# Layer 0 of a four-layer graph network on one core: the first chunk's norm taken in two pairs of tiles

## The chip, the cores and the metric

One Trainium2 chip, one of its cores. The metric is the device time of one execution of the whole kernel in microseconds (us); several executions are summed up by their median.

## The reference, cut to what matters

The kernel runs four layers over `x` (128 sequences of 64 nodes with 256 features, fp32). Each layer is `x = x + layer(relu(layernorm(x)))`. The change lies in the first stage of layer 0 alone:

```python
h = jnp.maximum(_layernorm(x, axis=-1), 0.0)
# layer 0
h = jax.nn.relu(jnp.einsum('ts,bsh->bth', adj, h @ Wg0 + bg0))
h = jax.nn.relu(jnp.einsum('ts,bsh->bth', adj, h @ Wg1 + bg1))
# then four LSTMs over windows of 1, 2, 3 and 4 nodes of h, and the residual
```

Layers 1 to 3 (attention over edges, a graph convolution with batch norm, attention over all nodes) are not touched.

## The kernel before, in words

The 8192 tokens are cut into 16 chunks of 512, each held as a tile `xin` of 128 partitions x 4 tiles x 256 features. `graph_convolutions(n)` is a generator that takes chunk n through layer 0's two graph convolutions in five stages, with a `yield` after each; the loop behind it advances several chunks by one stage per turn, so that their stages interleave. The stages of a chunk:

1. The norm. On VectorE (DVE) `bn_stats` and `bn_aggr` for each of the four tiles (L96, L97); on ScalarE (ACT) one square root over the four variances (L104); on DVE a reciprocal (L105) and one `scalar_tensor_tensor` that makes the bias (L106); on ACT four `Relu` activations with scale and bias (L120, `scaled`). The result is `h`.
2. `aggregate`: 8 matmuls of `h` with the block matrix `bdA` (two copies of the transposed adjacency) on TensorE (PE, L51), and two DVE copies of 128x512 out of PSUM into `aggT` (L171).
3. Four matmuls with `Wg0` (L51, `bank<-aggT,wg`); for each half a DVE operation (L624) that adds `rsum` times `bg0` and a `Relu` on ACT (L632), giving `h1T`.
4. Eight matmuls with `Wg1` and two DVE additions of `bg1` (L647).
5. Eight matmuls with `bdA`, two `Relu` on ACT (L663) into the tile that the LSTMs read.

An fp32 matmul of the program shows as two MATMUL records in the profile.

Ahead of chunk 0 PE runs products of a tile of ones with itself (`turn_over`, L57: 4 matmuls, then the row sums of the adjacency into a PSUM bank at L600, then 8 more); DVE copies the row sums out into `rsum` (L602).

The loads. SyncE's queue (SP) issues, in order: the four tiles of chunk 0 (L576), chunk 1 (L569), `Wg0` (L582), `Wg1` (L586), chunks 2 and 3 (L569), two LSTM biases (L591, L592), chunk 4, and then what the tables of layer 1 need: first `acol` (L308, 1 KB), then eight small pieces `ahalf` (L313), the edge lists, further chunks. ACT's queue issues the adjacency, transposed (`adjT`, two halves) and plain (`adj`, two halves, L579), `bg0` (L584, 1 KB) and `bg1` (L588, one row of 1 KB read for each of the 128 partitions). Chunk 4 goes into the buffer of chunk 0, so its load is issued when the last of chunk 0's four activations at L120 has read it. The loads of SP and ACT take eight semaphores in turn, and a load waits until the eighth load before it has landed.

The tables of layer 1 (`edge_tables`) are built by DVE operations that are strewn between those of the graph convolutions. Among them is `diag_a` at L346, two operations that multiply the identity by a column of `acol`.

Order on an engine: the framework's scheduler places instructions; those given to `late` (`keep_in_program_order`) keep their order among themselves. Each engine runs its own list strictly in order and waits at an instruction until its semaphores are there. The statistics (`stats`) and the activations (`scaled`) of the norms are kept in program order; the roots (L104 to L106), the copies L171 and the table operations are placed by the scheduler.

Of the kernel before, what the change touches and what calls it, by code (L numbers as in the profile page):

```python
# [9 lines left out]
F32 = mybir.dt.float32  # L10
# [3 lines left out]
AF = mybir.ActivationFunctionType  # L14
ALU = mybir.AluOpType
AX = mybir.AxisListType

P = 128
T = 64
# [12 lines left out]
def gnn_stack_kernel(ctx: ExitStack, tc: tile.TileContext, a: dict, out: bass.AP):  # L32
    nc = tc.nc
# [6 lines left out]
    stat = ctx.enter_context(tc.tile_pool(name="stat", bufs=4))  # L40
# [3 lines left out]
    def bank():  # L44
        return psums["now"].tile([P, 512], F32, tag="bank", name="bank", bufs=psums["banks"])
# [4 lines left out]
    def mm(o, lhsT, rhs, start=True, stop=True):  # L50
        nc.tensor.matmul(o, lhsT, rhs, start=start, stop=stop)  # L51

    def turn_over(lhsT, rhs, times):

        p = bank()
        for _ in range(times):
            late(nc.tensor.matmul(p[:, : rhs.shape[-1]], lhsT, rhs, start=True, stop=True))  # L57
# [17 lines left out]
    eps = const.tile([P, 1], F32, tag="eps", name="eps")  # L75
    nc.vector.memset(eps, 1e-5)

    def late(ins):

        tc.keep_in_program_order(ins)  # L80
# [4 lines left out]
    class Norm:  # L85
# [13 lines left out]
        def roots(self):  # L99
            mv = self.mv  # L100
            rs = self.rs = stat.tile([P, 4], F32, tag="ln_rs", name="ln_rs")
            nm = self.nm = stat.tile([P, 4], F32, tag="ln_nm", name="ln_nm")
            if self.root_on_scalar:
                nc.scalar.activation(rs, mv[:, :, 1], AF.Sqrt, bias=eps)  # L104
                nc.vector.reciprocal(rs, rs)  # L105
                nc.vector.scalar_tensor_tensor(nm, mv[:, :, 0], -1.0, rs, ALU.mult, ALU.mult)  # L106
            else:
                first = nc.gpsimd.tensor_scalar(rs, mv[:, :, 1], 1e-5, None, ALU.add)
                if self.known:
                    self.keep(first)  # L110
                nc.gpsimd.tensor_tensor(rs, rs, half_power, ALU.pow)
                nc.gpsimd.tensor_tensor(nm, mv[:, :, 0], rs, ALU.mult)
                nc.gpsimd.tensor_scalar(nm, nm, -1.0, None, ALU.mult)

        def scaled(self, i):

            if self.h is None:
                self.h = hpool.tile([P, 4, D], F32, tag="h", name="h")
            self.keep(
                nc.scalar.activation(  # L120
                    self.h[:, i, :],
                    self.xt[:, i, :],
                    AF.Relu,
                    bias=self.nm[:, i : i + 1],
                    scale=self.rs[:, i : i + 1],
                )
            )
# [37 lines left out]
    def aggregate(h, bd, dst):  # L165

        for c in range(2):
            p = bank()
            for i in range(4):
                mm(p[:, i * P : (i + 1) * P], h[:, i, c * P : (c + 1) * P], bd)  # L170
            nc.vector.tensor_copy(dst[:, c, :], p)  # L171
# [314 lines left out]
    with ExitStack() as l0:  # L486
# [60 lines left out]
        bias = w0.tile([P, MAX_SKIP, 8], F32, tag="bias", name="bias")  # L547
        bias2 = w0.tile([P, MAX_SKIP, 8], F32, tag="bias2", name="bias2")
        ones = w0.tile([P, P], F32, tag="ones", name="ones")
# [4 lines left out]
        with ExitStack() as conv:  # L554
# [12 lines left out]
            def load_x(n):  # L567
                xt = xin.tile([P, 4, D], F32, tag="xin", name="xin")
                nc.sync.dma_start(out=xt, in_=token_tiles(a["x"], n))  # L569
                return xt  # L570
# [10 lines left out]
            wg0 = wc.tile([P, 2, D], F32, tag="wg0", name="wg0")  # L581
            nc.sync.dma_start(out=wg0, in_=a["Wg0"])  # L582
            bg0 = wc.tile([P, 2], F32, tag="bg0", name="bg0")
            nc.scalar.dma_start(out=bg0, in_=a["bg0"])  # L584
            wg1 = wc.tile([P, 2, D], F32, tag="wg1", name="wg1")
            nc.sync.dma_start(out=wg1, in_=a["Wg1"])  # L586
            bg1 = wc.tile([P, D], F32, tag="bg1", name="bg1")
            nc.scalar.dma_start(out=bg1, in_=a["bg1"].partition_broadcast(P))  # L588
            for n in (2, 3):
                coming[n] = load_x(n)  # L590
            nc.sync.dma_start(out=bias, in_=a["bih"])  # L591
# [6 lines left out]
            rsum = wc.tile([P, T], F32, tag="rsum", name="rsum")  # L598
            p = bank()
            late(nc.tensor.matmul(p[:, :T], ones[:T, :], adjT2[:T, :], start=True, stop=True))  # L600
            turn_over(ones, ones, 8)
            nc.vector.tensor_copy(rsum, p[:, :T])  # L602
            rsum_b = rsum.unsqueeze(1).to_broadcast([P, 8, T])

            def graph_convolutions(n):

                norm = Norm(coming.pop(n), True)
                for i in range(4):
                    norm.stats(i)
                    if n == 1 and i == 1:  # L610
                        yield
                h = norm.finished()
                if 4 <= n + 3 < NCH:
                    coming[n + 3] = load_x(n + 3)
                yield
                aggT = g0.tile([P, 2, CHUNK], F32, tag="aggT", name="aggT")
                h1T = g0.tile([P, 2, CHUNK], F32, tag="h1T", name="h1T")
                aggregate(h, bdA, aggT)
                yield
                for c in range(2):  # L620
                    p = bank()
                    for k in range(2):
                        mm(p, wg0[:, k, c * P : (c + 1) * P], aggT[:, k, :], k == 0, k == 1)
                    nc.vector.scalar_tensor_tensor(  # L624
                        h1T[:, c, :].rearrange("p (b t) -> p b t", t=T),
                        rsum_b,
                        bg0[:, c : c + 1],
                        p.rearrange("p (b t) -> p b t", t=T),
                        ALU.mult,
                        ALU.add,  # L630
                    )
                    nc.scalar.activation(h1T[:, c, :], h1T[:, c, :], AF.Relu)  # L632
                yield
                z = aggT.rearrange("p c t -> p (c t)").rearrange("p (i d) -> p i d", i=4)
                for ip in range(2):
                    p = bank()
                    for i2 in range(2):
                        i = 2 * ip + i2
                        for k in range(2):
                            mm(  # L640
                                p[:, i2 * D : (i2 + 1) * D],
                                h1T[:, k, i * P : (i + 1) * P],
                                wg1[:, k, :],
                                k == 0,
                                k == 1,
                            )
                    nc.vector.tensor_tensor(  # L647
                        z[:, 2 * ip : 2 * ip + 2, :],
                        p.rearrange("p (i d) -> p i d", i=2),
                        bg1.unsqueeze(1).to_broadcast([P, 2, D]),  # L650
                        ALU.add,
                    )
                yield
                if n < NCH // 2:
                    col = n % 2 * CHUNK
                    dst = hTs0[n // 4][:, n % 4 // 2, :, col : col + CHUNK]
                else:
                    dst = hop.tile([P, 2, CHUNK], F32, tag="hop", name="hop")
                for c in range(2):
                    p = bank()  # L660
                    for i in range(4):
                        mm(p[:, i * P : (i + 1) * P], z[:, i, c * P : (c + 1) * P], bdA)
                    nc.scalar.activation(dst[:, c, :], p, AF.Relu)  # L663
                if n >= NCH // 2:
                    nc.sync.dma_start(out=hmem[n], in_=dst)
# [341 lines left out]
        for slot in range(len(tasks) + 2):  # L1007
# [33 lines left out]
            if new:  # L1041
# [4 lines left out]
                if step.w == MAX_SKIP and step.t == 2 and k < 2 and step.g < NGR - 1:  # L1046
                    for u in range(2):
                        n = 4 * step.g + 2 * u + k
                        later.append((slot, "x", n))
            while later and later[0][0] <= slot:  # L1050
                _, kind, n = later.pop(0)
# [28 lines left out]
    with ExitStack() as l1:  # L1080
# [32 lines left out]
        for g, c, u, ip in last_outs:  # L1113
            if not ip:
                n = 4 * g + 2 * u + c
# [523 lines left out]
    with ExitStack() as l2:  # L1639
# [55 lines left out]
        with ExitStack() as dense2:  # L1695
# [67 lines left out]
            with ExitStack() as first_dense:  # L1763
# [43 lines left out]
                for slot, (pr, m2) in enumerate(tasks):  # L1807
                    n = slot + 3
                    if slot == NCH - 5:
# [3 lines left out]
                            out=early[:, 0, : 2 * P].rearrange("p (q m) -> p q m", q=2),  # L1813
                            in_=a["W2T"].rearrange("p (q k) (j m) -> p k q j m", q=2, j=2)[:, 0, :, 1, :],
# [569 lines left out]
```

## Time and profile before

| what | us |
|---|---|
| three runs | 1938.48, 1938.86, 1939.79 |
| median | 1938.86 |
| the profiled execution's own time | 1934.87 |
| its span, first to last instruction | 1933.1 |
| PE busy in it | 1909.7 (99%) |
| DVE, ACT, GpSimd (POOL) busy | 1320.9, 1166.4, 435.7 |

The profiled execution is 3.99 us below the median of the three runs. Rows of the timeline read: start in us from the span's start, duration in us, engine, source line, operation, output <- inputs, shape, count, and in brackets the engine's idle time before the row and what ended it. An engine with the letter q (SPq, ACTq) is its queue issuing a DMA. PEld is PE's weight load, which overlaps with PE.

### The profile page before, as it was taken

Reading aid. Unit: us, or ns where it says so; the run is one execution under the profiler, and the core shown is the slowest. Engines: PE = TensorE matmul, PEld = TensorE weight load, DVE = VectorE, ACT = ScalarE, POOL = GpSimd, SP = SyncE. Lnnn points to the kernel's source line nnn. Section 1 sums busy time; section 2 is a strip of 40 time slices with the busy share of each in tenths; the row PEclk is TensorE's granted clock in tenths of the full one; section 3 lists DMA queues with packets and bytes.
Section 4 is the critical chain, followed back from the end, with each engine's and each line's share of the span. In section 5 each row is a group of like instructions: output and inputs, shape, how many; then the busy total and the mean of one; then the engine's idle time right before and its main releaser. Section 6 shows DMA issues by size and latency. Waiting matters only on the chain. (4 is left out here: it accounts for less than half of the span.)

```text
span 1933.1 us, 25259 instructions
## 1 busy us (share of the span) xinstructions
PE 1909.7 (99%) x9146; PEld 1395.2 (72%) x9146; DVE 1320.9 (68%) x2531; ACT 1166.4 (60%) x2200; POOL 435.7 (23%) x622
## 2 busy tenths in 40 slices
PE   9999999999999999999999999999999999999998
PEld 7777468876678874688766788876676875444787
DVE  8774675674565557755745655688788877787886
ACT  4353775664565547756645656488886656592654
POOL 0333021110010000211100100066776520000584
PEclk9999999999999999999999999999999999999999
DMA  8846010010010035100100100242323841022112
GB/s 278 297 170 219 0 39 0 1 77 0 1 77 1 1 135 203 39 1 1 77 0 1 61 1 16 96 171 95 136 69 116 326 162 57 1 77 78 43 66 88
DMA packets 67212, 158.25 MB, mean 82 GB/s; under 512 B 6928, under 2 KB 41872, under 8 KB 64784
## 3 DMA queue, kind: packets, MB, share of 16 engines
q1 hardware_dynamic: 60272, 127.87, 18.8%
q0 software_dynamic: 6208, 28.58, 4.0%
q8 instruction: 72, 1.18, 0.2%
q14 instruction: 52, 0.43, 0.1%
q10 hardware_dynamic: 608, 0.20, 0.1%
HBM read 98.95 MB, written 57.68 MB: 81 GB/s over the span
## 5 line engine op out<-in xcount | busy, mean ns | idle before, releaser
L800 PE MATMUL pa<-xop,wih 128*128 128x256 f32 (+2 forms) x1376 | 442.8, 412 | 2.3 <-DVE gate L854 1.9
L828 ACT ACTIVATE gate<-gate,bias 128x256 f32<-128x256 f32 (+2 forms) x368 | 247.8, 678 | 170.6 <-DVE gate L844 86.8
L800 PEld LDWEIGHTS pa<-xop,wih 128*128 128x128 f32 x1376 | 259.2, 190 | 87.7 <-issue 19.8
L800 PE MATMUL pa<-lstm_h,whh 128*128 128x256 f32 (+1 forms) x896 | 283.6, 398 | 0.0
L800 PE MATMUL pc<-xop,wih 128*128 128x256 f32 (+2 forms) x736 | 251.1, 423 | 0.0
L844 DVE TENSOR_TENSOR gate<-pb,gate 128x256 f32<-128x256 f32 (+2 forms) x184 | 87.6, 476 | 228.2 <-PE pb L800 159.5
L800 PEld LDWEIGHTS pa<-lstm_h,whh 128*128 128x128 f32 x896 | 170.2, 190 | 40.2
L772 POOL COPY xop<-hT 128x256 f32<-128x256 f32 (+1 forms) x36 | 30.0, 833 | 655.2 <-DVE gate L851 278.8
L800 PEld LDWEIGHTS pc<-xop,wih 128*128 128x128 f32 x736 | 139.8, 190 | 51.2 <-issue 22.5
L861 DVE TENSOR_TENSOR gate<-pc,gate 128x256 f32<-128x256 f32 (+2 forms) x184 | 87.8, 477 | 117.7 <-PE pc L800 116.8
L1210 ACT ACTIVATE lr<-pair 128x1024 f32<-128x1024 f32 x128 | 124.2, 1023 | 39.9 <-ACT xv L1194 16.8
L800 PE MATMUL pc<-lstm_h,whh 128*128 128x256 f32 (+1 forms) x448 | 141.8, 398 | 0.0
L843 ACT COPY gate<-pa 128x256 f32<-128x256 f32 (+2 forms) x184 | 76.0, 413 | 86.7 <-PE pa L800 86.5
L1175 PE MATMUL bank<-wlv,hT 128*128 128x260 f32 x480 | 115.6, 382 | 1.7 <-DVE xq L1186 1.7
L854 DVE TENSOR_TENSOR gate<-pa,gate 128x256 f32<-128x256 f32 (+2 forms) x184 | 87.7, 476 | 41.2 <-PE pa L800 40.5
L828 ACT ACTIVATE gate<-pa,bias 128x256 f32<-128x256 f32 (+2 forms) x184 | 93.8, 510 | 30.6 <-PE pa L800 28.4
L848 ACT COPY gate<-pa 128x256 f32<-128x256 f32 (+2 forms) x184 | 75.2, 409 | 56.2 <-PE pa L800 55.3
L800 PE MATMUL pb<-xop,wih 128*128 128x256 f32 (+1 forms) x320 | 101.7, 399 | 1.4 <-POOL xop L772 1.2
L1175 PEld LDWEIGHTS bank<-wlv,hT 128*128 128x128 f32 x480 | 88.2, 190 | 16.6 <-DVE xq L1186 3.6
L800 PEld LDWEIGHTS pc<-lstm_h,whh 128*128 128x128 f32 x448 | 85.1, 190 | 20.1
L851 ACT COPY gate<-pc 128x256 f32<-128x256 f32 (+2 forms) x136 | 57.9, 426 | 53.2 <-PE pc L800 53.1
L1216 DVE SCALAR_TENSOR_TENSOR lr<-lr,fold 128x1024 f32<-128x1024 f32 x64 | 82.7, 1293 | 3.7 <-ACT lr L1210 1.7
(391 smaller groups left out, 3706.5 us busy)
## 6 DMA issues: line engine op xcount, KB each, us to landing
wih<-qih SPq DMA_DIRECT2D x6, 1792.0 KB, 10.5
field<-keep SPq DMA_DIRECT2D x4, 2304.0 KB, 11.1
whh<-qhh SPq DMA_DIRECT2D x5, 1792.0 KB, 7.2
xres<-in_x SPq DMA_DIRECT2D x16, 512.0 KB, 4.7
xa<-xres POOLq DMA_DIRECT2D x16, 512.0 KB, 4.0
xin<-xb SPq DMA_DIRECT2D x16, 512.0 KB, 3.3
h<-xb SPq DMA_DIRECT2D x16, 512.0 KB, 3.3
xin<-in_x SPq DMA_DIRECT2D x15, 512.0 KB, 5.8
```

What stands on the lines that cost most here:

```text
L772: copy(self.as_nodes(v[:, to : to + 1]), self.nodes(slice(k, k + 1), t))
L800: ins = nc.tensor.matmul(p[:, : self.N], weights[kind, self.phase](k, q), x[k], start=first_ and kind == "ih", stop=kind == "hh" or not se ...
L828: nc.scalar.activation(out, in_, AF.Tanh if q == 2 else AF.Sigmoid, bias=bias[:, self.w - 1, 2 * q + j : 2 * q + j + 1],)
L843: nc.scalar.copy(blk[0, 0], pa[:, :N])
L844: nc.vector.tensor_tensor(blk[0, 0], pb[:, :N], blk[0, 0], ALU.add)
L848: nc.scalar.copy(blk[1, 0], pa[:, :N])
L851: (nc.vector.tensor_copy if not self.t and self.w > 1 else nc.scalar.copy)(blk[1, 1], pc[:, :N])
L854: nc.vector.tensor_tensor(blk[1, 1], pa[:, :N], blk[1, 1], ALU.add)
L861: nc.vector.tensor_tensor(blk[1, 0], pc[:, :N], blk[1, 0], ALU.add)
L1175: ins = nc.tensor.matmul(o, hTs[n][:, k, i * P : (i + 1) * P], wlv[:, k, cols], start=k == 0, stop=k == 1)
L1210: nc.scalar.activation(lr, p, AF.Relu)
L1216: late(nc.vector.scalar_tensor_tensor(lrs[1], lrs[0], fold, lrs[1], ALU.mult, ALU.add))
```

## The change

For chunk 0 alone the norm is written out: the statistics of tiles 0 and 1, one square root over these two, the statistics of tile 2, reciprocal and bias of the first pair, activation 0, the statistics of tile 3, the square root of the second pair, activation 1, reciprocal and bias of the second pair, activations 2 and 3, all kept in program order. The copy of `rsum` is put behind them and kept in order too. The second `turn_over` has 6 matmuls in place of 8. `bg0` and `bg1` are issued by GpSimd's queue instead of ACT's.

```diff
+        def root_pair(self, ip, part):
+            if ip + part == 0:
+                self.rs = stat.tile([P, 4], F32, tag="ln_rs", name="ln_rs")
+                self.nm = stat.tile([P, 4], F32, tag="ln_nm", name="ln_nm")
+            i2 = slice(2 * ip, 2 * ip + 2)
+            rs, nm, mv = self.rs[:, i2], self.nm[:, i2], self.mv[:, i2]
+            if part == 0:
+                self.keep(nc.scalar.activation(rs, mv[:, :, 1], AF.Sqrt, bias=eps))
+            else:
+                self.keep(nc.vector.reciprocal(rs, rs))
+                self.keep(nc.vector.scalar_tensor_tensor(nm, mv[:, :, 0], -1.0, rs, ALU.mult, ALU.mult))
...
-            nc.scalar.dma_start(out=bg0, in_=a["bg0"])
+            nc.gpsimd.dma_start(out=bg0, in_=a["bg0"])
...
-            nc.scalar.dma_start(out=bg1, in_=a["bg1"].partition_broadcast(P))
+            nc.gpsimd.dma_start(out=bg1, in_=a["bg1"].partition_broadcast(P))
...
-            turn_over(ones, ones, 8)
-            nc.vector.tensor_copy(rsum, p[:, :T])
+            turn_over(ones, ones, 6)
+            rsum_bank = p
...
-                for i in range(4):
-                    norm.stats(i)
-                    if n == 1 and i == 1:
-                        yield
-                h = norm.finished()
+                if n == 0:
+                    norm.stats(0)
+                    norm.stats(1)
+                    norm.root_pair(0, 0)
+                    norm.stats(2)
+                    norm.root_pair(0, 1)
+                    norm.scaled(0)
+                    norm.stats(3)
+                    norm.root_pair(1, 0)
+                    norm.scaled(1)
+                    norm.root_pair(1, 1)
+                    norm.scaled(2)
+                    norm.scaled(3)
+                    h = norm.h
+                    late(nc.vector.tensor_copy(rsum, rsum_bank[:, :T]))
+                else:
+                    for i in range(4):
+                        norm.stats(i)
+                        if n == 1 and i == 1:
+                            yield
+                    h = norm.finished()
```

The built programs differ in order over the first 130 or so of DVE's instructions and nowhere behind them; PE's list differs by the two matmuls left out, and in that chunk 0's eight matmuls of `aggregate` stand half by half instead of tile by tile. On DVE the scheduler now places the first `diag_a` ahead of chunk 1's last `bn_aggr`, and the second between chunk 1's reciprocal and its bias:

```
before: bn_stats, bn_aggr, L624, reciprocal L105, bias L106, bn_stats, diag_a, bn_aggr, bn_stats, L624, bn_aggr, bn_stats, diag_a
after:  bn_stats, diag_a, bn_aggr, L624, reciprocal L105, diag_a, bias L106, bn_stats, bn_aggr, bn_stats, L624, bn_aggr
```

The rows begin with the statistics of chunk 1's last tile. On SP's queue the order of the first 20 loads stays, but two loads fewer take part in the turn of the eight semaphores: chunk 1 now waits for the first half of `adjT` instead of chunk 0's first tile, and `acol` for chunk 1 instead of `bg1`. On GpSimd the two loads stand ahead of the copies that fill `bdA` (L595).

## The prediction

> **What bounds the kernel now.** I read the page first, then PE's waits and timeline over the first 45 us, then the timelines of DVE, ACT and SP there, then the DMA view in stretches.
>
> ```profile
> PE 1909.7 (99%) x9146; PEld 1395.2 (72%) x9146; DVE 1320.9 (68%) x2531; ACT 1166.4 (60%) x2200; POOL 435.7 (23%) x622
> ```
>
> PE is the bound; only its idle time can be won or lost. PE's waits of the first 150 us:
>
> ```profile
> PE bank L57 <- DVE ones L550: 1.2, 1, 1.2
> PE bank L51 <- ACT h L120: 0.8, 2, 0.5
> PE bank L51 <- DVE aggT L171: 0.6, 1, 0.6
> PE bank L424 <- DVE wide L420: 0.2, 1, 0.2
> PE bank L51 <- ACT h1T L632: 0.2, 1, 0.2
> ```
>
> PE's rows place them: all but the 0.2 us at L424 end by 17.25, and from there PE runs without a gap for 70 us.
>
> ```profile
> 3.81 3.65 PE L57 MATMUL bank<-ones 128*128 128x128 f32 x16
> 7.97 2.09 PE L51 MATMUL bank<-bdA,h 128*128 128x128 f32 x16 [0.51 <-ACT h L120]
> 10.63 3.70 PE L51 MATMUL bank<-aggT,wg 128*128 128x512 f32 x8 [0.56 <-DVE aggT L171]
> 14.61 0.71 PE L51 MATMUL bank<-bdA,h 128*128 128x128 f32 x4 [0.28 <-ACT h L120]
> 17.25 3.29 PE L51 MATMUL bank<-wg,h1T 128*128 128x256 f32 x14 [0.16 <-ACT h1T L632]
> ```
>
> So the price of this change is how much later or earlier PE reaches the row at 17.25; all behind it moves along. What feeds these rows on DVE (and, last two rows, ACT):
>
> ```profile
> 7.94 0.43 DVE L96 BATCH_NORM_STATS2 ln_st<-xin 128x6 f32<-128x256 f32 x1 [0.75 <-DMA xin<-in_x]
> 9.88 1.29 DVE L171 COPY aggT<-bank 128x512 f32<-128x512 f32 x2 [0.16 <-PE bank L51]
> 12.65 0.75 DVE L624 SCALAR_TENSOR_TENSOR h1T<-rsum,bg,bank 128x512 f32<-128x512 f32 x1 [0.28 <-PE bank L51]
> 13.31 0.17 DVE L105 RECIPROCAL ln_rs<-ln_rs 128x4 f32<-128x4 f32 x1
> 15.20 0.29 DVE L346 TENSOR_SCALAR diag_a<-ident,acol 128x128 f32<-128x128 f32 x1 [1.18 <-DMA acol<-in_a]
> 15.40 0.18 DVE L97 BATCH_NORM_AGGREGATE ln_mv<-ln_st 128x2 f32<-128x6 f32 x1
> 15.49 0.40 DVE L96 BATCH_NORM_STATS2 ln_st<-xin 128x6 f32<-128x256 f32 x1
> 13.43 0.63 ACT L632 ACTIVATE h1T<-h1T 128x512 f32<-128x512 f32 x1 [0.73 <-DVE h1T L624]
> 13.97 2.06 ACT L120 ACTIVATE h<-xin,ln_nm,ln_rs 128x256 f32<-128x256 f32 x4
> ```
>
> Two waits for loads stand here: chunk 1's data at 7.94 and `acol` at 15.20. The second costs little now, because all that chunk 1's matmuls at 14.61 need is ahead of it. The DMA totals from 7 to 9.5 us with its two queues (q10 is ACT's), then from 9.5 to 14:
>
> ```profile
> DMA packets 454, 0.59 MB, mean 237 GB/s; under 512 B 46, under 2 KB 284, under 8 KB 454
> q1 hardware_dynamic: 307, 0.46, 50.8%
> q10 hardware_dynamic: 147, 0.13, 30.9%
> DMA packets 1875, 1.51 MB, mean 336 GB/s; under 512 B 462, under 2 KB 1844, under 8 KB 1875
> ```
>
> The DMA is a backlog: `acol`, issued at 9.79, lands 5.4 us later, just behind chunk 4 (issued 9.33, 5.7 us).
>
> **Chunk 0's norm.** The two issues of 0.60 and 0.44 us leave ACT's queue, so the table load of 1.28 us starts at 3.25 instead of 4.36 and ends at 4.53. Tile 0 lands at 2.9 (issued at 0.72, 2.2 us), DVE is through its long memsets at 2.82; two tiles of statistics at some 0.6 us each with a memset between (4.06 to 5.22 before) are done at 4.4. Root 4.53 to 4.83; from its end to the first activation it was 0.44 (6.79 to 7.23), plus 0.2 for the third tile's statistics in between: activation 0 at 5.5. Tile 3's statistics end about 6.0; the second root runs behind activation 0 to 6.35, plus 0.44: activation 2 at 6.8, activation 3 from 7.3 to 7.9. It ended at 9.30 before: 1.4 us earlier. The two matmuls left out (4 of 16 records in 3.65 us, 0.9 us) ran in PE's waiting time; PE then starts at 6.5 and has half 0 done by 8.3 instead of 9.8.
>
> **Where that gain goes.** On DVE the `aggT` copies stand behind chunk 1's first statistics, four table operations and the `rsum` copy, and those statistics wait for chunk 1's load. In the rows that is 7.94 to 9.72, with 0.16 us idle before the copies at 9.88. So the copies can come at most 0.16 us earlier however early PE is. Chunk 1's load now waits for the `adjT` half (in at 3.16, where PE's L600 starts at 3.19) and not for tile 0: issued at 3.2 instead of 2.98, it lands near 8.1. Copies at 10.0, `Wg0` matmuls at 10.75 instead of 10.63. The 1.4 us shrink to -0.1 or +0.1. The second, small extra root, reciprocal and bias (0.30, 0.18, 0.16 us) lie in the same cover.
>
> **The wait that moves forward.** After the copies (1.3 us), two rows of statistics: DVE is at the first `diag_a` at about 12.3, and there it now stands ahead of chunk 1's last `bn_aggr`, of L624, reciprocal and bias, which release ACT's root, its `Relu` L632 and chunk 1's activations, which release PE. From `acol`'s landing A: `diag_a` 0.20 to the next row (15.20 to 15.40), `bn_aggr` 0.1: L624 at A+0.3. It ends at A+1.05, L632 starts at A+1.08 (12.65 to 13.43 was 0.78). The bias L106 comes at A+1.24: L105 0.66 after L624 (12.65 to 13.31), then 0.28 for the second `diag_a` between. Activation 0.54 behind L632 (13.43 to 13.97): A+1.62. PE 0.64 behind it (13.97 to 14.61): A+2.26. The 0.16 us at 17.25 are absorbed, as the second L624 is not held again. So PE's shift is A + 2.26 - 0.16 - 14.61 = A - 12.51.
>
> **When `acol` lands.** It is queued behind chunk 4, whose issue comes earlier (activation 3 ends at 7.9, not 9.30), but the backlog sets the end. Upper end: the same bytes over the same engines, A = 15.2, shift +2.7. Lower end: from 5.2 us, 2.65 MB (chunks 1 to 4, `Wg0`, `Wg1`, biases) at the best slice's 385 GB/s take 6.9, and 0.9 us lie between the last data and the landing (14.3 to 15.2): A = 13.0, shift +0.5. In between: with q10 gone from 7 to 9.5, where `bg1` was read, q1 could move 336 GB/s x 2.5 us = 0.84 MB instead of 0.46, worth 1.1 us, less the 0.2 of chunk 1's later issue. A = 14.3, shift **+1.8**. I take that, as it is nearest to rows of this stretch. Behind 17.25 the feeding operations keep their leads over PE (`aggT` ready at 18.98, needed at 20.37; the next activations start at 19.22, needed at 23.81), and DVE is held less long than PE is shifted, so nothing is added.
>
> **GpSimd's queue.** Two issues of 0.53 to 0.80 us (the first three of its kind, at 78.6 us) stand ahead of the `bdA` copies at 3.28 and 3.99, in idle time of 1.46 us, and PE wants `bdA` at 6.5: nothing, until each takes 2 us more. `bg0` is first read by L624 near 14.6, `bg1` by L647 near 21 (19.40 before): ten us of cover.
>
> **The clock.** The 16 dummy records up to 7.46 take 3.65 us, 16 of the same shape at 23.81 take 1.95: PE starts at half rate and is fast by 8 us. The change makes PE idle from 14.3 to 16.6, 2.3 us, where the longest idle time of before is the 1.2 us of the first wait shown; whether the rate falls, no row shows. Bounds: nothing, or as long a slow stretch as at the start, 1.19 to some 7.2, 6 us at half rate, 3.0 us lost. I take nothing, since 2.3 is nearer to the gaps of up to 1.2 behind which rows keep their length.
> The Trainium skill ("TensorE: Matmul & The Clock Gate", section "HAM oscillation") asks for no PE-idle gaps over some 3.4 us; by that rule 2.3 us would cost nothing, and a gap past it would add an estimated 1.7 us (half of one 3.4 us window).
>
> **Sum.** 1934.87 + 1.8 = 1936.7 for the profiled execution; carried to the median of the runs, 3.99 higher: 1938.86 + 1.8 = **1940.7**. That is 0.09%; about 0.2% (3.9 us) is what a measurement of this kernel can tell from no change.
>
> **Rivals.**
> *No hold*: `acol` lands before DVE asks for it (12.3), or chunk 1's load comes before 7.8. Then -0.1 to, at the very most, the 1.4 us by which `h` is early: 1937.5 to 1938.8. For it: q10 leaves q1 alone. Against it: the lower bound of A is 13.0. Chance 0.10.
> *Slow clock*: the forecast's hold, and PE falls to half rate behind it: +1.8 + 3.0 = +4.8, 1943.7. It decides once the slow stretch is over 4.2 us (2.1 us lost). For it: PE's lead-in is shorter by 0.9 us and its idle time twice the longest of before. Chance 0.14.
> *The change doesn't do what it says*: chunk 0's `h` is not early because `bg1` on the DMA engines from 2 to 4 us delays tiles 2 and 3. Up to 1.0 us of delay leaves the forecast as it is, since the copies wait for chunk 1; beyond, `Wg0` and with it nothing before A is late. Price 0.
>
> **How the numbers follow.** Forecast 0.76 (A from 13.0 to 15.2: 1939.4 to 1941.6, and a us on each side, as three runs spread over 1.3). The range of 1938.0 to 1943.7 takes in the slow clock's centre and leaves out most of *no hold*. Faster by over 0.2%: 0.03. Slower: 0.17, the slow clock and a part for what the rows don't show. Same: 0.80.
>
> **What would show it.** `h` done near 7.9 and the `aggT` copies still near 10; DVE idle some 2 us before `diag_a`, ended by `acol` near 14.3; PE idle over 2 us before chunk 1's matmuls near 16.6; no new gap behind. Wrong if DVE isn't held there, if PE's 128x512 records behind the hold are over 0.6 us apart, or if the shift at 45 us differs from that at the end.

## The result and the profile after

| what | before | after |
|---|---|---|
| median of the runs on one chip | 1939.05 (22 runs) | 1941.92 (22 runs) |
| lowest and highest | 1938.48, 1942.29 | 1940.63, 1945.63 |
| the profiled execution's own time | 1934.87 | 1941.91 |
| its span | 1933.1 | 1940.1 |

The ratio of the times is 1.0014, with an interval of 1.0008 to 1.002: the change costs 1.6 to 3.9 us, 2.9 by the medians. That is below the 0.2% that the prediction took for what a measurement can tell, but the whole interval is on the slow side. The profile shows where it is lost. Line numbers are higher now: by 13 for the loads, the copies (L184), `diag_a` (L359) and the activations that make `h` (L133), by 29 for L653 (L624 before).

PE's two waits that grew, in its waits from 0 to 150 us (us in total, times, longest):

```profile
PE bank L51 <- ACT h L133: 2.7, 2, 1.8
PE bank L51 <- DVE aggT L184: 1.7, 1, 1.7
```

They were 0.8 and 0.6. PE's timeline of the kernel after places them:

```profile
7.93 2.41 PE L51 MATMUL bank<-bdA,h 128*128 128x128 f32 x14 [0.87 <-ACT h L133]
12.08 3.70 PE L51 MATMUL bank<-aggT,wg 128*128 128x512 f32 x8 [1.74 <-DVE aggT L184]
17.60 0.71 PE L51 MATMUL bank<-bdA,h 128*128 128x128 f32 x4 [1.82 <-ACT h L133]
19.92 3.19 PE L51 MATMUL bank<-wg,h1T 128*128 128x256 f32 x14
26.38 1.95 PE L51 MATMUL bank<-bdA,h 128*128 128x128 f32 x16
```

The last of these rows is chunk 2's. Before it was:

```profile
23.81 1.95 PE L51 MATMUL bank<-bdA,h 128*128 128x128 f32 x16
```

`Wg0` starts at 12.08 instead of 10.63, chunk 1's matmuls at 17.60 instead of 14.61. Chunk 2's start at 26.38 instead of 23.81, and that 2.57 us stays the shift of PE's rows for hundreds of us; below I call it the steady shift. It compares one profiled execution with another. What feeds them on DVE, and the last of chunk 0's activations on ACT:

```profile
6.41 0.43 DVE L96 BATCH_NORM_STATS2 ln_st<-xin 128x6 f32<-128x256 f32 x1 [0.83 <-DMA xin<-in_x]
9.41 0.43 DVE L96 BATCH_NORM_STATS2 ln_st<-xin 128x6 f32<-128x256 f32 x1 [1.49 <-DMA xin<-in_x]
11.34 1.28 DVE L184 COPY aggT<-bank 128x512 f32<-128x512 f32 x2
15.38 0.29 DVE L359 TENSOR_SCALAR diag_a<-ident,acol 128x128 f32<-128x128 f32 x1 [1.90 <-DMA acol<-in_a]
7.29 1.61 ACT L133 ACTIVATE h<-xin,ln_nm,ln_rs 128x256 f32<-128x256 f32 x3
```

Three loads are late here. Tile 3 of chunk 0 comes at 6.41, so `h` is done at 8.90: 0.4 us earlier than before, not 1.4. Chunk 1 comes at 9.41 (7.94 before). And DVE stands at `diag_a` for 1.90 us until `acol` lands. The DMA view from 4 to 6.5 us shows what competes with the first two (queue: packets, MB, share of the 16 engines). Before, then after, where q0 is GpSimd's queue:

```profile
q1 hardware_dynamic: 493, 0.49, 75.4%
q10 hardware_dynamic: 126, 0.02, 4.2%
```

```profile
q0 software_dynamic: 45, 0.13, 46.2%
q1 hardware_dynamic: 320, 0.31, 40.6%
```

`bg1` is read in this stretch now, and SP's queue q1, which carries tiles 2 and 3 and chunk 1, moves 0.31 MB instead of 0.49. In the packet records bg1 was 128 packets of 1 KB on ACT's queue from 6.95 us on, 96 ns each, 12.3 us of engine time; on GpSimd's queue it is 32 packets of 4 KB from 4.13 us on, 573 ns each, 18.3 us.

All runs together bear this out for chunk 1, but not for tile 3. In the five profiled executions with the early read (after, and e1, e3, e6 and e8 below) DVE's first statistics of chunk 1 run at 9.19 to 10.10 us; in the six without it at 7.60 to 8.68. Tile 3's statistics had to wait for their load in after and e8 (6.41 and 7.01), but with the same early read they ran without such a wait at 5.66 to 5.84 in e1, e3 and e6. So what delayed tile 3 is not shown.

### The profile page after: what moved, and what is told of

It is laid out like the page before. It is cut to its first block, busy times and chain, and to the rows that moved or that the text cites. A ratio compares the mean times of both kernels' runs of the same rounds, so it can differ in the third digit from the quotient of the medians.

```text
span 1940.1 us, 25258 instructions
## 1 busy us (share of the span) xinstructions
PE 1911.5 (99%) x9142; PEld 1395.7 (72%) x9142; DVE 1323.1 (68%) x2533; ACT 1166.5 (60%) x2201; POOL 436.9 (23%) x624
```

## The experiments

**Which of the two waits is the loss.** e1 takes the wait for `acol` off DVE's list by keeping the two `diag_a` operations where they are written, behind chunk 1's norm:

```diff
-                nc.vector.tensor_scalar(diag[:, c, :], ident, acol[:, c : c + 1], None, ALU.mult)
+                late(nc.vector.tensor_scalar(diag[:, c, :], ident, acol[:, c : c + 1], None, ALU.mult))
```

> The changed kernel, with the two diag_a operations kept in program order, so that they stand some 45 places later on DVE and nothing of chunk 1 is queued behind the wait for acol. Loads as in the changed kernel. Theory 1 (DVE is held at diag_a by acol): chunk 1's first matmuls are then set by the late Wg0 matmuls: 12.08 + 3.98 (10.63 to 14.61 in the kernel before) = 16.1 instead of 17.60; PE's steady rows are +1.1 to +1.45 us behind the kernel before, down from +2.57; about 1940.3 us where the kernel before has 1939.05. Theory 2 (only the loads that bg1 delays cost time): the place of diag_a is of no account, the shift stays at +2.6, 1941.7 us.

Measured: 1941.98 us where before has 1939.26, ratio 1.0012 (1.0002 to 1.0021). The wait for `acol` is gone and the loss is not: 2.7 us, the number of the second theory. The first theory's 1940.3 was missed. Chunk 1 landed at 10.10 in the profiled execution, the copies ran at 12.04, and PE waited for them. PE's `Wg0` row, and the windows behind (busy us and count of PE, PEld, DVE, ACT, POOL; then PE's granted clock, DMA share, GB/s):

```profile
12.78 5.25 PE L51 MATMUL bank<-aggT,wg 128*128 128x512 f32 x8 [3.18 <-DVE aggT L184]
```

```profile
9.10:12.52 3.42, 0.49 (x5) 0.30 (x3) 2.32 (x10) 0.00 (x0) 0.00 (x0) 1.00 1.10 360
12.52:15.93 3.41, 3.15 (x4) 1.51 (x5) 1.80 (x6) 0.30 (x1) 0.00 (x0) 0.50 0.33 88
```

The eight records took 5.25 us instead of 3.70: behind a window with PE busy for 0.49 us the clock was granted at one half for one window. So the steady shift of 3.28 in this execution is 1.7 us of late copies (2.15 at `Wg0`, less the 0.42 that is absorbed) and 1.55 of clock. It is a long execution, 1943.75, the second longest of eleven, and PE falls back by another 1.8 us near 195 us; the sizes are its own. The rows say that the loss has two sources: with the wait for `acol` away, the late landing of chunk 1 takes its place. The runs below test that.

**The queue alone, and the norm alone.** e2 is the kernel after with both small loads back on ACT's queue (the pairs and the hold stay); e3 is the kernel before with both on GpSimd's (the early read and, by the scheduler's order, the hold); e4 is e2 with e1's edit, so the two pairs and the shorter `turn_over` by themselves.

```diff
e2, e4:
-            nc.gpsimd.dma_start(out=bg0, in_=a["bg0"])
+            nc.scalar.dma_start(out=bg0, in_=a["bg0"])
-            nc.gpsimd.dma_start(out=bg1, in_=a["bg1"].partition_broadcast(P))
+            nc.scalar.dma_start(out=bg1, in_=a["bg1"].partition_broadcast(P))
e3: the same two lines the other way, in the kernel before
```

> The changed kernel, with bg0 and bg1 back on ACT's queue; diag_a stays ahead of chunk 1's last bn_aggr. Theory 1: tiles 2 and 3 land by 5.0, chunk 1 near 7.9, the aggT copies come at 9.9, the Wg0 matmuls at 10.6, and DVE is still held by acol, which lands at 15.2: shift 15.2 - 12.5 = +2.3 to +2.7 us; 1941.5 us. Theory 2: with the loads on time the loss is gone, shift 0 or below, 1939 us or less.

> The kernel before, with bg0 and bg1 on GpSimd's queue and nothing else; the scheduler places diag_a ahead of chunk 1's last bn_aggr here too. Theory 1: the hold is there without the pairs: acol lands at 15.2 to 15.4, shift +2.4 to +2.9 us; 1941.7 us. Tile 3 and chunk 1 land 1.5 us late as in the changed kernel, so the norm's last activation ends about 10.5. Theory 3 (the pairs of roots are what costs): shift 0, 1939 us.

> The changed kernel, with diag_a kept in program order as in e1 and bg0 and bg1 on ACT's queue as in e2: the norm in pairs alone, without the hold and without the early bg1. Theory 1: h is ready 0.8 to 1.2 us earlier, but the aggT copies wait for chunk 1's statistics and its load at 7.9: copies at 9.7 to 9.9, shift -0.2 to 0 us; 1939 us. Rival: the pairs carry through, copies at 8.5, shift -1.2 us; 1937.8 us.

| | median | ratio (interval) | `diag_a` held till | chunk 1's matmuls | steady shift |
|---|---|---|---|---|---|
| e2 | 1943.55 | 1.0019 (1.001 to 1.0028) | 15.29 | 17.44 | 2.41 |
| e3 | 1943.01 | 1.0019 (1.001 to 1.0028) | 15.64 | 17.86 | 2.83 |
| e4 | 1939.09 | 1.0001 (0.9992 to 1.001) | not held | 15.21 | 0.18 |

Before was 1939.26 on this chip. Each half of the change alone brings the hold (the scheduler puts `diag_a` ahead of chunk 0's first `h1T` operation in both), and each alone costs no less than the two together did. In e3 the norm's last activation ended at 9.30, as before, not at the expected 10.5. With neither the hold nor bg1's early read, in e4, the pairs neither gain nor lose; the edit from e2 to e4 takes away the hold alone.

The medians of e2 and e3 lie 4.3 and 3.8 us above before, 1.9 and 0.9 more than their steady shifts; both profiled executions are among the fastest of their kernel (1941.50 and 1941.46). In e2 a part of that may be the clock: its five executions with a mean granted clock of 0.998 have a median of 1943.95, the other six 1941.94. The profiled one lost a window too, ahead of the hold, where it cost nothing in the end:

```profile
5.51:8.92 3.41, 2.25 (x13) 1.51 (x13) 2.43 (x11) 2.81 (x7) 0.00 (x0) 1.00 0.82 267
8.92:12.34 3.42, 3.42 (x12) 2.73 (x13) 2.33 (x9) 0.00 (x0) 0.00 (x0) 0.50 1.06 359
```

What the rest of the two differences is stays open. DVE and PE in e4 show why the pairs bring no gain:

```profile
8.68 0.43 DVE L96 BATCH_NORM_STATS2 ln_st<-xin 128x6 f32<-128x256 f32 x1 [0.91 <-DMA xin<-in_x]
11.23 3.70 PE L51 MATMUL bank<-aggT,wg 128*128 128x512 f32 x8 [1.04 <-DVE aggT L184]
```

`h` is ready 0.84 us earlier for PE there, but the copies stand behind chunk 1's statistics, and these wait for their load, which came at 8.68 here, later than before.

**A control and another way to take the hold away.** e5 puts e1's edit into the kernel before; e6 is the kernel after with `acol` issued by ACT's queue, so that it is there before DVE asks for it. Both ran on another chip, where before has a median of 1935.97.

```diff
e6:
-            nc.sync.dma_start(out=acol, in_=a["a1"])
+            nc.scalar.dma_start(out=acol, in_=a["a1"])
```

> The kernel before with one edit: the two `diag_a` scalings keep the place in which they are written, as in e1 and e4. It is the control for these two. Theory 1 (the 1.18 us that VectorE waits there in the kernel before lies in a gap of PE's work that other waits set anyway): steady shift of PE's rows within 0.1 us of 0, time 1938.9 to 1939.4 us. Theory 2 (the wait costs something before, too, and e4's gain of h was seen too small or too large for it): shift -0.3 to -1.0 us, time 1938.2 to 1938.8 us.

> The kernel after, with `acol`'s load as the third on ScalarE's queue, behind adjT's two halves and ahead of adj's, or near there; the wait at `diag_a` is gone because its data is early, not because the instruction is moved behind others. Theory 1 (two separate costs, the hold for acol and the late landing of chunk 1 behind bg1's read): the hold is gone, chunk 1 lands at 9.4 to 10.1 us, PE's chunk 1 matmuls start 6.65 us behind that as in e1 without its half-clock window, so 16.1 to 16.8 us, steady shift +1.0 to +1.7 us, time 1940.1 to 1940.8 us; where a half-clock window falls behind PE's wait for chunk 0's copies, up to 1.6 us more. Theory 2 (all of the loss is the hold): shift within 0.3 us of 0, 1938.9 to 1939.4 us.

e5: 1936.10, ratio 1.0 (0.9991 to 1.0009), shift of chunk 1's matmuls 0.04, steady 0.23 (from 31 us on; from 20 to 28 us PE is 0.38 ahead, and loses it at a wait for `h1T`). The shift is outside the first theory's 0.1, the time is that of before: by the median, the place of `diag_a` is worth nothing there. e6: 1938.76, ratio 1.0016 (1.0007 to 1.0025). Its rows are near those of the first theory, chunk 1 at 9.19 (expected 9.4 to 10.1) and a steady shift of 1.22:

```profile
9.19 0.43 DVE L96 BATCH_NORM_STATS2 ln_st<-xin 128x6 f32<-128x256 f32 x1 [1.91 <-DMA xin<-in_x]
12.27 3.70 PE L51 MATMUL bank<-aggT,wg 128*128 128x512 f32 x8 [2.56 <-DVE aggT L184]
```

Its median is 2.8 us up, not 1.2. The profiled execution had no window at half clock behind PE's wait; it is also the shortest of the eleven (1936.40), and of the other ten six have a mean granted clock of 0.998 or less, which none of the 33 of before has. That fits a half-clock window in a part of the executions, as e1's profile shows one, but no execution of e6 shows it directly. The clock can't be all of it: the three executions with a mean clock of 1.0 have a median of 1938.12, still 2.2 us up.

**What sets the landing of `acol`.** e7 leaves out bg1's read (and so the second bias of layer 0), e8 takes three of chunk 4's four tiles out of the queue ahead of `acol`.

```diff
e7:
-            nc.gpsimd.dma_start(out=bg1, in_=a["bg1"].partition_broadcast(P))
+            nc.gpsimd.memset(bg1, 0.0)      # behind the copies into bdA
e8:
-                if 4 <= n + 3 < NCH:
+                if n == 1:
+                    coming[4] = xin.tile([P, 4, D], F32, tag="xin", name="xin")
+                    nc.sync.dma_start(out=coming[4][:, 0, :], in_=token_tiles(a["x"], 4)[:, 0, :])
+                elif 4 < n + 3 < NCH:
                     coming[n + 3] = load_x(n + 3)
...
                         next(tables, None)
+                        if n == 3 and one is turns[0]:
+                            nc.sync.dma_start(out=coming[4][:, 1:, :], in_=token_tiles(a["x"], 4)[:, 1:, :])
```

> The kernel after without bg1's load: GpSimd fills bg1 with zeros behind its bdA copies, so layer 0's second bias is left out of the result. It measures the term A with bg1's read wholly away. Theory 1 (A was mis-sized because bg1's read was not saved but moved ahead onto tiles 2 and 3 and chunk 1): tile 3 lands about 4.9 to 5.3 us, chunk 1 7.9 to 8.3 us, h is done about 7.9, acol lands 13.8 to 14.3 us, PE's chunk 1 matmuls at 16.0 to 16.5, steady shift +1.0 to +1.5 us, time 1940.1 to 1940.6 us. Theory 2 (acol lands late whatever bg1 does, since the loads of x4 and W_linT set it): acol 15.0 to 15.4 us, steady shift 2.2 to 2.6 us, time 1941.3 to 1941.7 us.

e7: 1938.38 against 1935.97, ratio 1.0012 (1.0003 to 1.0021). Half of each theory held. Without bg1's read chunk 1 is there when DVE asks for it (7.60) and `Wg0` starts at 10.26, the earliest of all these kernels. But `acol` still lands at 15.15:

```profile
15.15 0.29 DVE L359 TENSOR_SCALAR diag_a<-ident,acol 128x128 f32<-128x128 f32 x1 [3.23 <-DMA acol<-in_a]
17.30 0.97 PE L51 MATMUL bank<-bdA,h 128*128 128x128 f32 x4 [3.34 <-ACT h L133]
```

```profile
14.20:17.61 3.41, 0.31 (x2) 0.31 (x3) 2.42 (x9) 1.48 (x3) 0.00 (x0) 1.00 0.15 42
17.61:21.03 3.42, 3.42 (x16) 3.24 (x15) 1.74 (x8) 1.82 (x5) 0.00 (x0) 0.50 0.24 59
```

So what was won ahead of the hold is lost in it, and again a nearly idle window is followed by one at half clock (shift 2.70 at 17.30, 3.92 behind). The packets of `acol`, 128 of 8 bytes in 16 groups of eight, say what the landing hangs on. DVE goes on some 0.6 us behind the start of the last of them:

| us | median start of the packets | start of the last | `diag_a` |
|---|---|---|---|
| before | 14.14 | 14.58 | 15.20 |
| after | 13.45 | 14.80 | 15.38 |
| e7, without bg1's read | 12.89 | 14.55 | 15.15 |
| e8, three tiles fewer ahead | 12.43 | 13.69 | 14.39 |

The last eight start within 0.1 us of the last packet of chunk 4's load, in every one of these. With bg1's read out of 7 to 9.5 us the middle of the queue comes forward, by 0.69 us in the kernel after and by 1.25 in e7, and the last group does not. In e7 it came alone, 0.95 us behind all others. The records don't name the DMA engine; that the last group is one engine with a longer backlog is read from chunk 4's last packets there, which follow one another at 42 ns with none between. Why one engine is that far behind stays open. The scatter is large, too: between profiled executions with the same loads the last packet differs by 0.2 us (before 14.58, e5 14.36) and 0.6 us (after 14.80, e1 15.43, with chunk 4 issued 0.4 us later), so differences of that size in the landing are not resolved.

> The kernel after, but only the first of chunk 4's four tiles is loaded ahead of `acol` on SyncE's queue; its other three tiles are loaded behind the loads of `src` and `dst`. Everything ahead of acol on that queue stays as it is, bg1's early read on GpSimd's queue too. It asks what sets acol's landing A, after e7 had it at 15.15 us with bg1's read wholly away. Theory 1 (A is the end of the slowest DMA engine's share of what was issued ahead on the same queue, since in every run so far acol's last eight packets start within 0.1 us of the last packet of chunk 4's load, and one engine's share of three tiles is 24 packets of 1 KB, some 41 ns each): A falls by about 1.0 us to 14.2 to 14.5 us. Theory 2 (A is a fixed 6 us behind acol's issue near 9.4 us): A stays at 15.2 to 15.4 us. PE's chunk 1 matmuls: VectorE has one stats pair more between diag_a and the second root here, so A + 2.8 to 3.0 us: 17.0 to 17.5 us by Theory 1, 18.0 to 18.4 us by Theory 2.

e8 asked whether the landing follows what is queued ahead. 1941.61 against 1939.32, ratio 1.0011 (1.0001 to 1.002). `acol` landed at 14.39 although it was issued 0.5 us later than in the kernel after (9.40):

```profile
9.91 0.43 SPq L321 DMA_DIRECT2D acol<-in_a  x1
14.39 0.29 DVE L359 TENSOR_SCALAR diag_a<-ident,acol 128x128 f32<-128x128 f32 x1 [1.42 <-DMA acol<-in_a]
```

PE's chunk 1 matmuls started at 17.20. Both numbers are those of the first theory; a fixed time behind the issue would have given 15.9. Between the slowest engine and the total of bytes e8 doesn't decide: its 0.39 MB less at the 385 GB/s of the prediction are 1.0 us as well, and the median packet came forward as much (1.02 us) as the last one (1.11). What speaks against the total are the packets of after and e7: their median came forward and the last one did not. The Trainium skill ("DMA: Bandwidth & Descriptors", section "Why a DMA increments its semaphore by 16 and not by 1") says that a load has landed only once each of its engines has posted its own increment; the table above agrees, with `diag_a` 1.1 to 2.3 us behind the median start and 0.6 to 0.7 behind the last.

This execution had a half-clock window too, after a shorter wait: PE waited 1.62 us for `h`, in a window in which it was busy for half the time.

```profile
6.51:9.92 3.41, 1.74 (x11) 1.17 (x10) 1.53 (x7) 1.82 (x4) 0.00 (x0) 1.00 1.01 343
9.92:13.33 3.41, 3.08 (x12) 2.26 (x11) 2.99 (x11) 0.00 (x0) 0.00 (x0) 0.50 0.85 259
```

**Both costs away, with the pairs kept.** w1 is the kernel after with e1's edit, and bg1 issued by SP's queue behind the LSTM biases, so that its read is behind chunk 1's.

```diff
-            nc.gpsimd.dma_start(out=bg1, in_=a["bg1"].partition_broadcast(P))
...
             nc.sync.dma_start(out=bias2, in_=a["bhh"])
+            nc.sync.dma_start(out=bg1, in_=a["bg1"].partition_broadcast(P))
```

> The kernel after with two edits: the `diag_a` scalings keep the place in which they are written, and bg1's load is issued on SyncE's queue behind `bhh`, so that its read lies behind chunks 1 to 3 instead of ahead of them. Theory 1 (the norm's two pairs do gain once neither the hold nor bg1's read takes it back): tile 3 lands about 4.9, h is done 7.9 to 8.4, chunk 1 lands 7.4 to 8.0, chunk 0's copies 9.2 to 9.8, PE's chunk 1 matmuls 13.9 to 14.5, steady shift -0.2 to -0.8 us, time 1938.4 to 1939.0 us. Theory 2 (chunk 1's stats and the copies behind them hold PE whatever bg1 does, as in e4): steady shift 0 to +0.3 us, time 1939.1 to 1939.5 us.

1935.30 against 1935.97, ratio 0.9997 (0.9988 to 1.0006). `h` is done at 8.21, 1.1 us earlier than before, and it brings nothing that can be measured:

```profile
8.49 0.43 DVE L96 BATCH_NORM_STATS2 ln_st<-xin 128x6 f32<-128x256 f32 x1 [1.28 <-DMA xin<-in_x]
15.14 0.71 PE L51 MATMUL bank<-bdA,h 128*128 128x128 f32 x4 [0.28 <-ACT h L133]
```

Chunk 1 landed at 8.49, not at 7.4 to 8.0, the copies came behind its statistics at 10.43, and the steady shift is 0.12: the second theory. How much an early chunk 1 could add in this order e7 tells: with chunk 1 there at 7.60, `Wg0` started 0.37 us earlier than before. To win more by an early `h`, the copies would have to stand ahead of chunk 1's statistics on DVE; that was not tried. The 1.55 us of clock in e1 was not tested by itself either.

## Why the prediction was right, and where it was not

The forecast was +1.8 us for a hold at `diag_a`, 1940.7 in all. Measured were +2.57 in the profiled execution's steady rows and +2.9 by the medians, 1941.92, inside the range of 1938.0 to 1943.7. The mechanism, the hold, was right. That the number is in the range is in part luck: 1941.92 is above the 1941.6 that the prediction's latest landing of `acol` gives, and the room above that was there for a slow clock. Point by point:

- **The hold: right.** DVE stands at the first `diag_a` for 1.90 us and PE starts chunk 1's matmuls at A + 2.22 (forecast A + 2.26; 2.15 in e2 and e7, 2.22 in e3). Behind it 0.42 us are absorbed, not 0.16.
- **A, the landing of `acol`: the step that failed.** The forecast took 14.3, between 13.0 and 15.2; it was 15.38, beyond its own upper end. Its in-between was worked out by what q1 could move once bg1's read had left 7 to 9.5 us. q1 did move 0.91 MB there (0.84 expected, 0.46 before). Two things were wrong. The read was counted where it left and not where it arrived, although the diff only moves it to another queue, where it went ahead of chunk 1 and took half as much engine time again in these two profiles. And the landing follows the last group of packets: even without bg1's read, in e7, `acol` came 0.05 us earlier than before and 0.23 earlier than in the kernel after, where the term gave 0.9 (1.1 less 0.2); both lie within the scatter above. A total over a stretch gives the middle of the queue, which did come forward by 0.69 us. The lower end had a smaller slip: between the last data and the go-ahead it took 0.9 us, while chunk 4's last packet starts at 14.49 and DVE goes on at 15.20, 0.7. The forecast shift is too small by the 1.08 us of A, less the 0.26 that more was absorbed and the 0.04 of the path from A to PE: 0.78, where 0.77 were seen.
- **`h` at 7.9: 8.90.** The first root (4.54), the first activation (5.62, forecast 5.5) and the earlier table load are as worked out; tile 3 then came at 6.41. That is the third rival's delay, 1.0 us, and as it said it left the hold's end as it was; that bg1's read is its cause is not shown, as e1, e3 and e6 have the read and not the delay.
- **Copies near 10, `Wg0` at 10.75: 11.34 and 12.08.** That the copies stand behind chunk 1's load was right; that it lands near 8.1 was not (9.41), again bg1's read. In the kernel after the hold covers this. e1 and e6 show its price with the hold away: 1.2 to 1.7 us, and the half clock on top where it comes. The prediction's rival *No hold* priced that case at no loss or a small gain, and it would have been wrong by some 3 us.
- **GpSimd's queue: right for the issues, incomplete for the data.** The copies into `bdA` run at 3.22 and 3.97 as before. The cost was on the DMA engines.
- **The clock: nothing in the profiled execution, something in others.** PE's wait ahead of chunk 1 was 1.82 us, not 2.3 (by the prediction's own rows 2.1, as `Wg0` would have ended at 14.45). The kernel after's profiled execution has no window at half clock behind its 1.74 and 1.82 us of waiting; of its 22 runs nine have a mean granted clock of 0.998, with a median of 1942.10 against 1941.81 for the others. That mark is a poor count: the four profiled executions that hold one half-clock window (e1, e2, e7, e8) all read 0.999. The rule of the Trainium skill that the prediction quotes ("TensorE: Matmul & The Clock Gate", section "HAM oscillation") puts the limit at idle gaps of some 3.4 us. The runs differ from it: longest waits of 0.92 us (e2), 1.62 (e8), 3.18 (e1) and 3.34 (e7) were each followed by a window at half clock. The prediction's estimate of 1.7 us for one such window is near e1's 1.55.
- **"Wrong if the shift at 45 us differs from that at the end".** It does, 2.57 against 6.9, most of it gained from 1477 to 1525 us. But e4, whose median is that of before, goes from 0.18 to 4.13 in the same way. The difference lies in the profiled execution of before, the one that the prediction found 3.99 us under its median. The record says more than that: in after, e1 to e4 and e8 PE pauses four times there, 1.4 to 1.7 us in all, with no releaser in the profile, and in before and the four runs on the chip where before has 1935.97 (e5, e6, e7, w1) it doesn't. The 1934.87 of that profile, too, lies in that chip's range for before (1934.53 to 1938.38) and below all 22 runs here. So the 3.99 us look like a difference between chips; which chip that profile was taken on is not on record. Against e4 PE's last rows in the kernel after are 2.8 us later, near the 2.9 of the medians.

## What to carry to other kernels

A load that moves to another queue has to be entered twice in the sum, where it leaves and where it arrives, and the loads that it then passes are the ones to price. A small load at the end of a full queue landed here with the last group of its packets, 0.4 to 1.7 us behind their median start, so a total of bytes over a stretch was the wrong ruler for it; issue such a load ahead of the big ones (e6: no wait for it), or don't put its reader ahead of work that the bottleneck waits for (e4, w1). And where two waits lie in parallel, taking away one of them shows the other: test the two apart and together before one of them is called the cause.

## What the runs showed of the hardware

- PE's granted clock changes in steps of 3.41 us whose phase differs between executions (the first full-speed window began between 5.51 and 8.21 us). PE need not be idle for a whole step to lose it: of the steps above, those with 0.31 (e7), 0.49 (e1), 1.74 (e8) and 2.25 us (e2) of busy time were followed by a step at half clock, while steps with 1.57 us in e6 (10.43 to 13.84) and 1.69 us in the kernel after (10.22 to 13.64) were not. Busy time alone, as the profile counts it, does not separate them.
- One row of 1 KB, read once for each of 128 partitions, took 8.1 to 12.3 us of DMA engine time in 1 KB packets from ACT's queue (64 to 96 ns each in before, e2, e4 and e5, where SP's packets of the same size took some 50) and 14.1 to 18.3 us in 4 KB packets from GpSimd's (after, e1, e3, e6, e8).
- Of the 16 groups of packets of one tiny load on SP's queue, the first started 1.3 to 2.7 us ahead of the last (e5 1.33, e1 2.70).
